# The first entry's norm moved ahead of the border between two stages of a decoder kernel

## The chip, the cores and the metric

The kernel runs on one core of one Trainium2 chip. The metric is device time in microseconds (us), from several runs; beside it stands one profiled execution, whose trace gives every instruction of every engine. The engines are TensorE (PE: matrix products and transposes; its weight loads are listed apart as PEld), VectorE (DVE), ScalarE (ACT), GpSimd (POOL) and the DMA queues, most of them fed by SyncE (SP). Each engine takes its own instructions in order and waits on semaphores for the others.

## The reference

Two decoder layers work on x of shape 8 x 256 x 256 (eight entries b of 256 tokens, width 256) with a context ctx of 8 x 256 x 512. All in float32. In short:

```python
x = x + attn0(layernorm(x))                   # 16 heads of 16, rotary
x = x + xattn0(ctx, layernorm(x))             # keys and values are halves of ctx
x = x + experts0(layernorm(x))                # 8 experts, sinkhorn gates, top 32 tokens each
x = x + attn1(layernorm(x))                   # 16 heads of 16, rotary, causal
x = x + xattn1(layernorm(x), ctx)             # 16 heads of 64, projections of ctx, a null key
x = x + ffn1(layernorm(x))                    # top 1 of 8 experts plus a shared one

def layernorm(x):
    return (x - mean(x)) / sqrt(var(x) + 1e-5)

def xattn1(xn, ctx):
    q, (k, v) = xn @ Wq, split(ctx @ Wkv)     # 256 -> 1024, 512 -> 2 x 1024
    k, v = concat(null_k, k), concat(null_v, v)
    out = softmax(q k^T / 8) v @ Wout         # per head
    return layernorm(out, 1e-6) * ln_scale + ln_bias
```

The change lies where attn1 of the last entry ends and xattn1 of the first entry begins.

## The kernel before, in words

The tokens of an entry lie as two tiles of 128 partitions; `x` holds all of them in SBUF (`x[:, 2 * b + t, :]` is tile t of entry b).

**First stage.** 24 units run one behind the other: self attention and cross attention of layer 0, entry pair by entry pair (units 0 to 15), and the causal self attention of layer 1 (units 16 to 23, one per entry). The first layer's experts run as generators between them. A unit has four steps k (two groups of heads by two tiles of keys); in step (n, k) the main loop issues the scores of the next step, then a first list of small jobs, then `values(k)` (products of exponentials and values, line 367; behind an odd k `divided_T`, lines 383 to 393, turns and divides them on DVE), then a second list. The lists are the table `order_of_jobs`, and its order is the order on all engines: the stage is traced under `manual_schedule(engines=PINNED)`, PINNED being PE, DVE, ACT, POOL and SP. The jobs kx0 to kx3 and vx0 already compute the key products of the second stage for entry 0 (`keys_x`, copied by ACT at line 888) and the first of four parts of the value products (`vals_x`, product at line 278, copied by ACT at line 902). Part 1 stands behind the loop, then the output product of the last unit (`units[-1].out`, product line 278, residual add line 502), then parts 2 and 3. After that the pinned order is closed, and the first stage's memory pools: `aw` (called `work`, with tags such as `xn` and `xnT` in two buffers), `pads`, and the PSUM pools (`amm`, called `mm`: three banks). New pools of the second stage take their room.

**Second stage.** `null_cross_attention` computes xattn1 entry by entry. Its pool `d2` is again called `work`, its PSUM pool `xmm` is again `mm`. Only PE's order is written out here; a planner orders the other engines by simulated times. It starts with `layernorm_T(0, ...)`: statistics on DVE (lines 249, 250, 252), a power -1/2 on POOL (254), two scalings on DVE (258), four transposes on PE (287), a copy by ACT (290). Then `features` (products with wq_x, PE line 272, copies by ACT at line 1404), `tables_x` (byk and its sums on DVE, lines 829 and 836; nvs zeroed by POOL at line 847 and filled by DVE at 850; nvw on PE at line 856), `null_key`, and the differences of weights on DVE (`sums_of_weights`, line 1428) that the entries from 1 on need, since their projections are made with seven products instead of eight (`seven`). Then for each entry `weighted`: scores on PE (1535), exponentials on ACT (1539, four buffers), on POOL the sum of the two key tiles (`both`, line 1541), on PE the denominators from it (`den`, line 1550) and the value products (`ox`, line 1575), whose copies alternate between ACT and DVE (1583). The order on PE is: scores of four heads pairs ahead, then the `den` products of the block before, then `ox`. The pool `kvs` on the right side of SBUF holds keys and values of one entry; it is opened at step (20, 1), together with the loads of the second stage's weights.

**Third stage.** `token_experts` runs the last feed-forward with experts loaded by DMA per slot.

Of the kernel before, what the change touches and what calls it, by code (L numbers as in the profile page):

```python
# [29 lines left out]
F32 = mybir.dt.float32  # L30
# [9 lines left out]
P = 128  # L40
B, S, D = 8, 256, 256
# [116 lines left out]
def plain(  # L158
# [7 lines left out]
    small = ctx.enter_context(tc.tile_pool(name="small", bufs=4))  # L166
# [3 lines left out]
    x = const.tile([P, NT, D], F32, name="x")  # L170
# [58 lines left out]
    def pack(e):  # L229


        full, tail = FF // P, FF % P
        to = packs[e, :, : 2 * FIRST].rearrange("p (c f) -> p c f", c=2)
        w1, w3 = (a[f"L1_ffn_{n}_eDF"][e].rearrange("(c p) f -> p c f", p=P) for n in ("w1", "w3"))
        nc.sync.dma_start(to[:, :, :FF], w1)
        nc.sync.dma_start(to[:, :, FF : FF + tail], w3[:, :, full * P :])
        nc.sync.dma_start(to[:, :, FF + tail :], w3[:, :, : full * P])
        to, w2 = packs[e, :, 2 * FIRST :].rearrange("p (c d) -> p c d", d=D), a["L1_ffn_w2_eFD"][e]
        nc.sync.dma_start(to[:, :full, :], w2[: full * P].rearrange("(c p) d -> p c d", p=P))
        nc.sync.dma_start(to[:tail, full, :], w2[full * P :])  # L240


    def norm_stats(views, eps, pool, tag):

        n = len(views)
        st = pool.tile([P, 2, 6], F32, tag=f"{tag}st", name=f"{tag}st")
        mv = pool.tile([P, 2, 2], F32, tag=f"{tag}mv", name=f"{tag}mv")
        for i, v in enumerate(views):
            nc.vector.bn_stats(st[:, i, :], v)
            nc.vector.bn_aggr(mv[:, i, :], st[:, i, :])  # L250
        ve = pool.tile([P, 2], F32, tag=f"{tag}ve", name=f"{tag}ve")
        nc.vector.tensor_scalar(ve[:, :n], mv[:, :n, 1], eps, None, ALU.add)  # L252
        rs = pool.tile([P, 2], F32, tag=f"{tag}rs", name=f"{tag}rs")
        nc.gpsimd.tensor_tensor(rs[:, :n], ve[:, :n], mhalf[:, :n], ALU.pow)  # L254
        return mv, rs

    def normed(dst, src, mv, rs, i, engine=nc.vector):
        return engine.tensor_scalar(dst, src, mv[:, i, 0:1], rs[:, i : i + 1], ALU.subtract, ALU.mult)

    def layernorm_T(b, work, mm, bufs=2):  # L260

        xn = work.tile([P, 2, D], F32, tag="xn", name="xn", bufs=bufs)
        mv, rs = norm_stats([x[:, 2 * b + t, :] for t in range(2)], 1e-5, small, "ln")
        for t in range(2):
            last = normed(xn[:, t, :], x[:, 2 * b + t, :], mv, rs, t)
        return last, transposed(xn, work, mm, "xnT", bufs=bufs)
# [9 lines left out]
    def product4(out, lhsT, rhs, start, stop):  # L276
        for h in range(0, P, HP):
            nc.tensor.matmul(  # L278
                out[h : h + HP], lhsT[:, h : h + HP], rhs, start=start, stop=stop, skip_group_check=True
            )  # L280

    def transposed(rows, work, mm, tag, dst=None, bufs=2):

        ps = mm.tile([P, 2, 2 * P], F32, tag="mm", name="tr")
        for t in range(2):
            for c in range(2):
                nc.tensor.transpose(ps[:, c, t * P : (t + 1) * P], rows[:, t, c * P : (c + 1) * P], ident)
        if dst is None:
            dst = work.tile([P, 2, 2 * P], F32, tag=tag, name=tag, bufs=bufs)
        nc.scalar.copy(dst, ps)  # L290
        return dst
# [285 lines left out]
    work = first.enter_context(tc.tile_pool(name="aw", bufs=2))  # L577
    banks = ExitStack()
    mm = banks.enter_context(tc.tile_pool(name="amm", bufs=3, space=PSUM))
# [27 lines left out]
    def expert_tables():  # L607
        nc.sync.dma_start(gate, a["L0_ffn_gate_w"].rearrange("(c p) e -> p c e", p=P))
        nc.sync.dma_start(experts, a["L0_ffn_experts"].rearrange("e (c p) f -> p e c f", p=P))

    def zeros():
        zero = one.tile([P, D], F32, name="zero")
        nc.gpsimd.memset(zero, 0.0)
        nc.sync.dma_start(xs.rearrange("(s p) d -> p s d", p=P), zero.unsqueeze(1).to_broadcast([P, TILES, D]))
        nc.sync.dma_start(
            ye[COMMON * P :].rearrange("(s p) d -> p s d", p=P), zero.unsqueeze(1).to_broadcast([P, TILES - COMMON, D])
        )
        nc.sync.dma_start(yo.rearrange("(s p) d -> p s d", p=P), zero.unsqueeze(1).to_broadcast([P, TILES - COMMON + 1, D]))
        for e in range(E):
            nc.sync.dma_start(packs[e, FF % P :, 2 * FIRST + FF // P * D :], zero[FF % P :])  # L620
# [251 lines left out]
    def context(b):  # L872
        t = ctxs.tile([P, CTX // P, S], F32, tag="ctxT", name="ctxT")
        nc.sync.dma_start(t, a["ctx_T"][b].rearrange("(c p) t -> p c t", p=P))
        return t

    def key_room():
        return kvs.tile([P, nc8, S], F32, tag="kT", name="kTx")

    def value_room():  # L880
        return kvs.tile([P, 2, XH, XD], F32, tag="vx", name="vx")
# [8 lines left out]
    def vals_x(v, ctxT, i):  # L890
        t, hh = i // 2, 8 * (i % 2)
        ps = mm.tile([P, 8, XD], F32, tag="mm", name="vps")
        lo = (XH + hh) * XD
        for cc in range(CTX // P):
            product4(
                ps.rearrange("p h d -> p (h d)"),
                ctxT[:, cc, bass.ts(t, P)],
                wkv_x[:, cc, lo : lo + 8 * XD],
                cc == 0,
                cc == CTX // P - 1,  # L900
            )
        nc.scalar.copy(v[:, t, hh : hh + 8, :], ps)
# [126 lines left out]
    def run(n, k, late):  # L1029
        for job in slots[4 * n + k][late]:  # L1030
            jobs[job]()
# [27 lines left out]
    for n, u in enumerate(units):  # L1059
        if n == 1:  # L1060
            nc.sync.dma_start(sin1, a["sin_halves"].rearrange("(t p) d -> p t d", p=P))
            expert_tables()
        if n == 3:
            zeros()
        if n == 2:
            nc.sync.dma_start(wqkv1, a["l1_wqkv"].rearrange("(c p) f -> p c f", p=P))
            nc.sync.dma_start(wo1, a["l1_wo"].rearrange("(c p) f -> p c f", p=P))
        for m in range(n + 2, min(n + 6, len(units))):
            v = units[m]
            if m == n + (5 if v.__class__ is SelfAttention else 2) or not n and m < 5:  # L1070
                v.load()
        if n >= 4 and n % 2 == 0 and n < 20:
            pack(n // 2 - 2)
        for k in range(4):
            if k < 3:
                u.core.scores(k + 1)
            elif n + 1 < len(units):
                units[n + 1].core.scores(0)
            run(n, k, 0)
            u.core.values(k)  # L1080
            run(n, k, 1)
            if (n, k) == (20, 1):
                for left in ex:
                    assert next(left, None) is None
                wd, ctxs, kvs, wproj, wkv_x, wq_x, wout_x, nkrow, nvcol, lns, lnb = weights_x()
                ctxT0, kv0 = context(0), (key_room(), value_room())
        opening.close()
    vals_x(kv0[1], ctxT0, 1)
    for t in range(2):
        units[-1].out(t)  # L1090
    for i in (2, 3):
        vals_x(kv0[1], ctxT0, i)
    order.close()
    first.close()
    banks.close()
# [1 line left out]
    mm = banks.enter_context(tc.tile_pool(name="xmm", bufs=3, space=PSUM))  # L1097
# [189 lines left out]
    def routed_norm(b, work):  # L1287

        xn = work.tile([P, 2, D], F32, tag="y", name="xne", bufs=1)
        mv, rs = norm_stats([x[:, 2 * b + t, :] for t in range(2)], 1e-5, small, "ln")  # L1290
        for kept, v in zip(norms[b], (mv, rs)):
            nc.gpsimd.tensor_copy(kept, v)
        for t in range(2):
            normed(xn[:, t, :], x[:, 2 * b + t, :], mv, rs, t)
        return xn
# [94 lines left out]
    def null_cross_attention(phase):  # L1390
        work = phase.enter_context(tc.tile_pool(name="d2", bufs=2))
# [14 lines left out]
        def query_room():  # L1406
            return work.tile([P, nc8, S], F32, tag="qT", name="qTx", bufs=1)
# [291 lines left out]

        order = ExitStack()  # L1700
        order.enter_context(tc.manual_schedule(engines={mybir.EngineType.PE}))
        _, xnT = layernorm_T(0, work, mm, 1)
        (kT, v), qT = kv0, query_room()
        features(qT, wq_x, xnT, nc.scalar.copy)
        wn, nvw, hot8 = tables_x(wd, wq_x, wout_x, nkrow, nvcol, work, mm)
# [8 lines left out]
        for b in range(B):  # L1714
# [4 lines left out]
            if more:  # L1719
                _, xnT = layernorm_T(b + 1, work, mm, 1)  # L1720
# [25 lines left out]
            rs, old = reciprocals(b, den, en), en  # L1746
# [30 lines left out]
        with tc.manual_schedule(engines={mybir.EngineType.PE, mybir.EngineType.DVE}):  # L1777
            for i, _ in enumerate(quarter(1)):
                if i == 0:
                    xn = routed_norm(B - 1, work)  # L1780
# [7 lines left out]
    with ExitStack() as phase:  # L1788
        null_cross_attention(phase)
# [1217 lines left out]
```

## Time and profile before

| what | us |
|---|---|
| median of 3 runs | 1139.07 (1138.89 to 1139.7) |
| profiled execution | 1139.85 |
| its span, first to last instruction | 1138.0 |
| PE busy | 1096.0 (96%) |
| DVE busy | 613.5 (54%) |
| ACT busy | 450.9 (40%) |
| POOL busy | 427.4 (38%) |
| granted PE clock, mean | 0.994 of full speed |
| end of the last value product of the first stage | 430.78 |
| start of the first product of the features | 432.94 |

Lines of the profile read: start, length (both us), engine, line of the kernel, operation, output<-inputs with shapes, and how many instructions are merged into the line. In brackets stands the idle time ahead of it on its engine and which instruction ended it. Summaries of a line give the least, median and largest duration in ns.

### The profile page before, as it was taken

Reading aid. Unit: us, or ns where it says so; the run is one execution under the profiler, and the core shown is the slowest. Engines: PE = TensorE matmul, PEld = TensorE weight load, DVE = VectorE, ACT = ScalarE, POOL = GpSimd, SP = SyncE. Lnnn points to the kernel's source line nnn. Section 1 sums busy time; section 2 is a strip of 40 time slices with the busy share of each in tenths; the row PEclk is TensorE's granted clock in tenths of the full one; section 3 lists DMA queues with packets and bytes.
Section 4 is the critical chain, followed back from the end, with each engine's and each line's share of the span. In section 5 each row is a group of like instructions: output and inputs, shape, how many; then the busy total and the mean of one; then the engine's idle time right before and its main releaser. Section 6 shows DMA issues by size and latency. Waiting matters only on the chain. (4 is left out here: it accounts for less than half of the span.)

```text
span 1138.0 us, 34797 instructions
## 1 busy us (share of the span) xinstructions
PE 1096.0 (96%) x15154; PEld 718.0 (63%) x15154; DVE 613.5 (54%) x1645; ACT 450.9 (40%) x727; POOL 427.4 (38%) x488
## 2 busy tenths in 40 slices
PE   6979999999999999999999999999999999999996
PEld 3434455555555445676777777777775768888874
DVE  5557889899878438344434343525257672221213
ACT  4657776656444433232323232323233320232220
POOL 3436366446677423333333424242425133000013
PEclk9989999999999999999999999999999999999998
DMA  8082333231103300102010102010122045899924
GB/s 248 2 262 101 105 107 97 75 110 55 37 12 136 118 3 20 39 20 49 20 48 20 49 20 49 20 49 20 48 104 69 1 155 206 351 412 409 375 81 130
DMA packets 54754, 120.37 MB, mean 106 GB/s; under 512 B 9008, under 2 KB 38944, under 8 KB 50240
## 3 DMA queue, kind: packets, MB, share of 16 engines
q1 hardware_dynamic: 48416, 102.32, 26.3%
q0 software_dynamic: 3456, 12.73, 3.0%
q10 hardware_dynamic: 2720, 3.02, 0.8%
q8 instruction: 121, 1.98, 0.7%
q14 instruction: 41, 0.34, 0.1%
HBM read 105.83 MB, written 29.51 MB: 119 GB/s over the span
## 5 line engine op out<-in xcount | busy, mean ns | idle before, releaser
L341 ACT ACTIVATE pT<-st 128x1024 f32<-128x1024 f32 (+1 forms) x128 | 110.4, 915 | 74.0 <-PE st L330 70.1
L367 PE MATMUL o<-pT,padv 128*32 128x256 f32 (+1 forms) x1536 | 96.4, 367 | 7.1 <-DVE by_q L383 5.6
L1541 POOL TENSOR_TENSOR both<-pTx 128x512 f32<-128x512 f32 x64 | 87.4, 1393 | 21.0 <-ACT pTx L1539 19.1
L272 PE MATMUL h<-xrT,w 128*64 128x128 f32 (+1 forms) x1936 | 86.9, 250 | 1.5 <-issue 1.5
L272 PEld LDWEIGHTS h<-xrT,w 128*64 128x64 f32 x1936 | 84.3, 137 | 4.4 <-issue 2.1
L1170 DVE TENSOR_TENSOR midr<-sl,h 128x128 f32<-128x128 f32 x102 | 29.4, 288 | 101.0 <-PE h L272 68.8
L341 ACT ACTIVATE pT<-st,kbias 128x1024 f32<-128x1024 f32 x64 | 67.8, 1111 | 36.0 <-PE st L330 36.0
L367 PEld LDWEIGHTS o<-pT,padv 128*32 128x32 f32 x1536 | 44.6, 110 | 54.7 <-issue 19.1
L1539 ACT ACTIVATE pTx<-stx 128x1024 f32<-128x1024 f32 x64 | 62.5, 1023 | 31.7 <-PE stx L1535 28.4
L1169 ACT ACTIVATE sl<-h 128x128 f32<-128x128 f32 (+1 forms) x114 | 35.2, 310 | 95.9 <-PE h L272 56.8
L254 POOL TENSOR_TENSOR lnrs<-lnve,mhalf 128x2 f32<-128x2 f32 x48 | 35.5, 743 | 94.2 <-DVE lnve L252 86.6
L330 PE MATMUL st<-qm,kT 32*128 32x512 f32 (+1 forms) x512 | 66.8, 589 | 3.9 <-DVE seq L513 2.1
L278 PE MATMUL qk<-xnT,l_wqkv 128*32 128x256 f32 x1024 | 66.9, 384 | 0.0
L1535 PE MATMUL stx<-qTx,kTx 64*128 64x256 f32 x512 | 64.4, 391 | 2.1 <-ACT pTx L1539 2.1
L1575 PE MATMUL ox<-pTx,vx 128*32 128x256 f32 x1024 | 63.3, 380 | 0.0
L1630 POOL TENSOR_TENSOR oT<-oT,rs 128x512 f32<-128x512 f32 x30 | 37.2, 1271 | 62.5 <-DMA rs<-rd 62.5
L1535 PEld LDWEIGHTS stx<-qTx,kTx 64*128 64x128 f32 x512 | 46.1, 186 | 20.4 <-issue 7.0
L346 POOL TENSOR_SCALAR_AFFINE_SELECT pT<-pT 128x512 f32<-128x512 f32 x64 | 42.1, 672 | 41.5 <-ACT pT L341 41.2
L254 POOL TENSOR_TENSOR lxrs<-lxve,mhalf 128x2 f32<-128x2 f32 x8 | 5.6, 705 | 127.3 <-DVE lxve L252 127.3
L383 DVE STREAM_TRANSPOSE by_q<-o 128x512 f32<-128x512 f32 x48 | 34.0, 708 | 33.0 <-PE o L367 32.9
L1583 DVE COPY oT<-ox 128x512 f32<-128x512 f32 x16 | 11.0, 690 | 72.3 <-PE ox L1575 72.3
L1575 PEld LDWEIGHTS ox<-pTx,vx 128*32 128x32 f32 x1024 | 35.0, 110 | 21.4 <-issue 2.7
(394 smaller groups left out, 2280.3 us busy)
## 6 DMA issues: line engine op xcount, KB each, us to landing
w<-packs SPq DMA_DIRECT2D x22, 1408.0 KB, 7.9
w<-packs SPq DMA_DIRECT2D x22, 768.0 KB, 9.3
rs<-rd SPq DMA_DIRECT2D x16, 512.0 KB, 5.9
packs<-L_ffn_w_eDF SPq DMA_DIRECT2D x8, 704.0 KB, 7.6
packs<-L_ffn_w_eDF SPq DMA_DIRECT2D x8, 640.0 KB, 7.7
packs<-L_ffn_w_eFD SPq DMA_DIRECT2D x8, 640.0 KB, 8.1
wkv_x<-L_xattn_Wkv POOLq DMA_DIRECT2D x1, 4096.0 KB
ctxT<-ctx_T SPq DMA_DIRECT2D x8, 512.0 KB, 3.9
```

The source lines that it names most:

```text
L254: nc.gpsimd.tensor_tensor(rs[:, :n], ve[:, :n], mhalf[:, :n], ALU.pow)
L272: nc.tensor.matmul(out[h], lhsT[:, h], rhs, start=start, stop=stop, skip_group_check=True)
L278: nc.tensor.matmul(out[h : h + HP], lhsT[:, h : h + HP], rhs, start=start, stop=stop, skip_group_check=True)
L330: nc.tensor.matmul(st[:, r, :, :n], self.kT[rows, c, bass.ts(kt, P)], self.qm[rows, :, c, q0:], start=True, stop=True,)
L341: nc.scalar.activation(pT[:, :, :, :n], st[:, 2 * k : 2 * k + 2, :, :n], AF.Exp, scale=self.scale, **kb)
L346: nc.gpsimd.affine_select(out=pT[:, :, :, :P], in_=pT[:, :, :, :P], compare_op=ALU.is_ge, fill=0.0, base=0, pattern=[[0, 2], [0, 2], [1, P ...
L367: nc.tensor.matmul(o[HP * j : HP * j + HP, m, q0:], self.v_pad[:, kt, 8 * c + 2 * j + m, :], pTs[j // 2][:, j % 2, m, : S - q0], start=kt ...
L1535: nc.tensor.matmul(st[:, g, kt, :], kT[rows, c, bass.ts(kt, P)], qT[rows, c, :], start=True, stop=True)
L1539: nc.scalar.activation(pT, st, AF.Exp, scale=scale)
L1541: nc.gpsimd.tensor_tensor(both, pT[:, :, 0, :], pT[:, :, 1, :], ALU.add)
L1575: nc.tensor.matmul(o[at : at + HP, i, :], v[:, kt, 2 * (c2 + i) + g, lo : lo + HP], pT[:, g, kt, :], start=kt == 0, stop=kt == 1, skip_gro ...
L1630: engines[c2 % 4 // 2].tensor_tensor(oT[:, c2 : c2 + 2, :], oT[:, c2 : c2 + 2, :], rs[:, c2 : c2 + 2, :], ALU.mult)
```

## The change

The norm of entry 0 is taken out of the second stage and written into the pinned order of the first. Its statistics are issued behind step (23, 0) of the main loop, its two scalings behind step (23, 1), into a tile `xn0` of the first stage's pool `work` (tag `xn`). Its four transposes and their copy are issued between the parts 2 and 3 of the value products, with a PSUM bank of the first stage's `mm`; the result `xnT0` lies in the pool `kvs`, which grows by one tile of 2 KB per partition. The second stage takes `xnT0` as it is. `norm_stats`, `normed` and `transposed` are the helpers that `layernorm_T` calls too; the number of instructions stays the same.

```diff
             run(n, k, 0)
             u.core.values(k)
             run(n, k, 1)
+            if (n, k) == (23, 0):
+                xn0 = work.tile([P, 2, D], F32, tag="xn", name="xn")
+                mv, rs = norm_stats([x[:, t, :] for t in range(2)], 1e-5, small, "ln")
+            if (n, k) == (23, 1):
+                for t in range(2):
+                    normed(xn0[:, t, :], x[:, t, :], mv, rs, t)
...
     for t in range(2):
         units[-1].out(t)
-    for i in (2, 3):
-        vals_x(kv0[1], ctxT0, i)
+    vals_x(kv0[1], ctxT0, 2)
+    xnT0 = transposed(xn0, kvs, mm, "xnT0", bufs=1)
+    vals_x(kv0[1], ctxT0, 3)
     order.close()
     first.close()
     banks.close()
...
-        _, xnT = layernorm_T(0, work, mm, 1)
+        xnT = xnT0
         (kT, v), qT = kv0, query_room()
         features(qT, wq_x, xnT, nc.scalar.copy)
```

## The prediction

> **What bounds the kernel now.** I read the page's first two parts, then the stretch that the change touches (420 to 465 us), engine by engine in the timeline, then TensorE's waits behind it, and the idle time of the engines that the moved work goes to.
>
> Page, busy time by engine, and two rows of the table of busy time by stage (second stage, entries 1 and 2):
> ```profile
> PE 1096.0 (96%) x15154; PEld 718.0 (63%) x15154; DVE 613.5 (54%) x1645; ACT 450.9 (40%) x727; POOL 427.4 (38%) x488
> ...
> 500.00:558.00 58.00, 57.74 (x782) 42.41 (x780) 25.99 (x69) 18.74 (x31) 19.98 (x21) 1.00 0.13 34
> 558.00:616.00 58.00, 57.74 (x780) 42.43 (x780) 24.23 (x59) 18.77 (x30) 20.20 (x21) 1.00 0.13 34
> ```
> In the rows by stage: window, its length, then busy us (and instructions) of PE, its weight loads, DVE, ACT, POOL, then granted clock and DMA. TensorE (PE) is the bound: 57.74 of 58 us in every entry of the second stage, granted clock 1.00. Whatever moves PE's work in the first entry moves the end by as much, as long as PE then waits for nothing else.
>
> Timeline of PE at the border of the stages:
> ```profile
> 422.00 1.91 PE L278 MATMUL ao<-l_wo,attT 128*32 128x256 f32 x32
> 423.73 7.05 PE L278 MATMUL vps<-wkv_x,ctxT 128*32 128x512 f32 x64
> 431.48 0.66 PE L287 MATMUL tr<-ident,xn 128*128 128x128 f32 x4 [0.71 <-ACT vx L902]
> 432.94 7.13 PE L272 MATMUL fm<-xnT,wq_x 128*64 128x256 f32 x64 [0.80 <-ACT xnT L290]
> ```
> The last two parts of the value products are the 7.05 us; they end at 430.78 and the features start at 432.94. Between lie 0.71 us of waiting, 0.66 of transposes, 0.80 of waiting.
>
> ACT beside it (copies of the value parts 2 and 3, then of the transposes):
> ```profile
> 427.41 0.59 ACT L902 COPY vx<-vps 128x512 f32<-128x512 f32 x1 [4.58 <-PE vps L278]
> 430.84 0.58 ACT L902 COPY vx<-vps 128x512 f32<-128x512 f32 x1 [2.85 <-PE vps L278]
> 432.30 0.58 ACT L290 COPY xnT<-tr 128x512 f32<-128x512 f32 x1 [0.87 <-DVE tw L1428]
> ```
> Timeline of DVE from the last residual add on, and of POOL:
> ```profile
> 423.98 0.69 DVE L502 TENSOR_TENSOR x<-x,ao 128x512 f32<-128x512 f32 x1 [3.21 <-PE ao L278]
> 424.58 1.91 DVE L258 TENSOR_SCALAR xn<-x,lnmv,lnrs 128x256 f32<-128x256 f32 x2
> 426.41 2.35 DVE L829 TENSOR_TENSOR byk<-wq_x,nkrow 128x1024 f32<-128x1024 f32 x2
> ...
> 443.98 0.41 DVE L864 COPY nvw<-nvw 128x256 f32<-128x256 f32 x1
> ...
> 448.40 0.89 DVE L1428 TENSOR_TENSOR wout_x<-wout_x 128x128 f32<-128x128 f32 x4
> 454.11 0.69 DVE L1583 COPY oT<-ox 128x512 f32<-128x512 f32 x1 [4.83 <-PE ox L1575]
> ```
> ```profile
> 425.05 0.97 POOL L847 MEMSET nvs<- 128x1024 f32 x1
> 445.16 5.26 POOL L1541 TENSOR_TENSOR both<-pTx 128x512 f32<-128x512 f32 x1 [19.14 <-ACT pTx L1539]
> ```
> DVE runs without a gap from 423.98 to 449.29: the norm, then one stream (table products, then the differences of the weights) of 449.29 - 426.41 = 22.88 us. POOL's first pair sum takes 5.26 us where the median of its 64 is 1.278 (all instances of line 1541), and it ends at 450.42, 1.13 behind the end of that stream: while DVE runs adds of two SBUF operands back to back, POOL's add stands still.
>
> Who waits for POOL: PE behind it, and the instances of line 1541.
> ```profile
> L1541 POOL TENSOR_TENSOR both<-pTx x64: 1255/1278/5256, 445.2 to 862.5; 128x512 f32<-128x512 f32 x64
> ```
> ```profile
> 450.90 0.63 PE L1550 MATMUL den<-both,hot 128*32 128x256 f32 x4
> 451.70 0.41 PE L1550 MATMUL den<-both,hot 128*32 128x256 f32 x2 [0.17 <-POOL both L1541]
> ```
> This is the line that decides. The second pair sum ends at 450.42 + 1.25 = 451.67, and PE takes up the matmul that needs it at 451.70, after a wait of 0.17. So at 451.7 the first entry already hangs on the end of DVE's stream: PE has 0.17 us of nothing to spare there. A gain ahead of it is lost at this place unless DVE's stream ends sooner too, and a later stream costs its whole delay.
>
> **The change, part by part.**
>
> *Statistics and norm, 20 us sooner.* Statistics: DVE 2 x 0.40 (bn_stats) + 2 x 0.17 + 0.15, some 1.3 us, behind the add-up of step (23,0), where DVE has nothing between 403.47 and 411.56; POOL's power 0.7 us (684 ns median) behind the mask of 406.18, which ends at 407.41, with POOL's next work at 412.13; the two scalings 2 x 0.40 behind the residual add that ends at 414.1, with DVE's next work at 418.82. Nothing queued behind them is due. POOL's masks of 414.65 to 415.88 may hold up the scalings or be held: the value products that need the masks start at 417.27, so up to 1.4 us is covered. Cost on the path: 0. No DMA is moved; in the unpinned order of before the statistics already ran ahead of 366 us, so they take nothing off the border.
>
> *Transposes between parts 2 and 3.* Four at a total of 0.66, same as now; PE reaches them at about 427.3 and the third part ends at 430.78 + 0.66 = 431.44 (0.5 if they overlap the products better). Their copy (0.58 on ACT) lies under the third part. The context load on SP waits for the third part's end: 0.66 later, landing some 6 us behind, needed at 444.6: covered.
>
> *Features.* They no longer wait for a norm's transposes. What is late next is the copy of the third part: 431.44 + 0.06 + 0.58 = 432.08, so the features start at about 432.14 instead of 432.94: PE gains 0.80. That the first product of the second stage waits for this copy I take from the transposes of before, which stood until 431.48 for the copy that ended at 431.42, though by the tiles of the program another bank than the one copied there was theirs: the new banks wait for all of the old ones. If only one bank counted, the features would follow at 431.44 and the gain be 1.5.
>
> *DVE's stream.* The two scalings leave 424.58, so the stream could start there, 1.83 sooner. But its first writes go into rooms of the second stage, which are opened over the closed rooms of the first, and the moved rows now lie in a room of the first (tag xn), read by the moved transposes. In before the last reader of those rooms was the output product that ends at 423.91, which DVE had waited for anyway. If the new rooms wait for every reader of the old ones, DVE now stands from 424.67 until the transposes end, 427.3 + 0.66 + 0.07 = about 428.0. Queued behind: the whole stream, then POOL's pair sums, then PE. The trace of before does not show this wait, so both ends: no wait, stream at 424.67 (-1.74); full wait, stream at 428.0 (+1.6). I take the full wait: the compiled program of before lists, for the first writes into the new room, waits for the last mask on POOL and the last transposition of the heads on DVE, whose tiles lie at other addresses than those written. [...]
>
> *The sum.* DVE's stream ends at 428.0 + 22.88 = 450.9 instead of 449.29, the second pair sum at 453.3 instead of 451.67: PE's 0.80 are gone and it goes on 1.6 later than before. One relief: PE's lead brings POOL's first pair sum to 444.3, ahead of the copy of nvw (before at 443.98, then at 445.6), which reads PSUM; if POOL slips in there, it runs 1.26 us, holds DVE for 0.93, and of the two sums one is left to do behind the stream: 450.9 + 0.93 + 1.13 = 452.95, 1.3 later. I take +1.5. All behind it is PE-dense and shifts as one. Profiled execution: 1139.85 (span 1138.0 and 1.85 around it) becomes 1141.3; it lies 0.8 above the median of the runs, 1139.07, which becomes **1140.6**, +0.13%. A measurement of this kernel tells some 0.2% from no change, so this is "same".
>
> [...]
>
> **The rivals.**
>
> *A. DVE doesn't wait* (the rooms go by address, or DVE finds other work first). Stream at 424.67 to 426.4: the second sum ends at or before 451.67, PE keeps 0.2 to 0.8, up to 1.5 if the features don't wait either: 1137.6 to 1138.9, worked as 1138.3. For it: DVE is in time everywhere else; against: the wait lists above.
>
> [...]
>
> [...]
>
> *C. Another plan.* In the second stage only PE's order is written out; the planner orders the others anew. PE has at most 0.26 us of waiting per entry to give back, so a new order can gain under 2 us and lose more, for example an oT copy queued behind a product that comes late: 0.3 us an entry, eight entries, 1143.
>
> **How the numbers follow.** Forecast (+0.9 to +2.0) 0.52; A 0.20; a part of the wait, 0 to +0.9, 0.11; B 0.08; C 0.09 (0.06 of it slower). Under 1136.8 (faster by 0.2%) 0.03; over 1141.35 (slower by 0.2%): B, most of C and the upper edge of the forecast, 0.17; within 0.80. Range: from A's gain of 1.4, 1137.7, to C's 1143.0. The likeliest one's own range is 1140.0 to 1141.1.
>
> **What would show it.** Right: features start near 432.1; byk starts near 428.0, with DVE idle ahead of it and the transposes named; the first pair sums end behind the end of DVE's stream near 451; PE waits over 1 us for POOL at line 1550. Wrong: byk at 424.7 (A), byk's first product over 2 us (B), or entries of the second stage whose length is no longer 57.7 us (C).

## The result, and the profile after

| | before, us | after, us |
|---|---|---|
| median, 6 runs each | 1139.25 (1138.89 to 1140.3) | 1135.45 (1132.62 to 1136.18) |
| profiled execution | 1139.85 | 1136.18 |
| its span | 1138.0 | 1134.6 |

The ratio is 0.996, with a 95% interval of 0.9946 to 0.9973. Two repeats later, each with its own runs of the kernel before, gave 0.995 (0.9935 to 0.9965) and 0.9961 (0.9949 to 0.9973). The change made the kernel faster by 0.4 to 0.5%, 4 to 6 us; the forecast was 1140.6, slower by 1.5.

The gain lies in three stretches, and only one of them is the border. Busy time by stretch, kernel before and then changed kernel (window, its length, then busy us and instructions of PE, its weight loads, DVE, ACT, POOL, then granted clock, DMA share, GB/s):
```profile
357.00:380.00 23.00, 21.01 (x341) 10.79 (x336) 14.44 (x43) 9.64 (x17) 15.36 (x22) 1.00 0.83 311
425.00:465.00 40.00, 38.07 (x454) 22.34 (x447) 28.62 (x69) 14.74 (x20) 14.95 (x10) 1.00 0.05 15
845.00:880.00 35.00, 34.02 (x296) 18.44 (x292) 25.60 (x37) 13.58 (x17) 22.52 (x33) 1.00 0.45 139
```
```profile
357.00:380.00 23.00, 22.64 (x371) 12.12 (x364) 14.66 (x38) 11.37 (x18) 16.01 (x24) 1.00 0.72 278
425.00:465.00 40.00, 39.04 (x470) 22.61 (x462) 34.05 (x68) 14.61 (x20) 15.36 (x10) 1.00 0.05 15
845.00:880.00 35.00, 34.74 (x320) 19.82 (x318) 19.21 (x38) 14.44 (x19) 21.06 (x33) 1.00 0.46 139
```
PE is fuller in all three after the change: 22.64 of 23 us instead of 21.01, 39.04 of 40 instead of 38.07, 34.74 of 35 instead of 34.02. Between the second and the third it is as full as before.

To size them, the rest of the document uses lengths between fixed PE instructions of one profile, so that nothing depends on how late a profile is at the first of them:

- I, first stage: from the `v` product that waits for the residual add of line 779 (361.79 in before) to the output product `ao` of the last unit (422.00).
- II, border: from there to the first key product of entry 1 (460.95).
- III, the rest of the second stage: from there to the transposes of `xne` in the last entry (864.89).

| profile | I | II | III |
|---|---|---|---|
| before, first and second profile | 60.21, 60.19 | 38.95, 38.95 | 403.94, 403.95 |
| changed, three profiles | 57.87, 57.87, 57.88 | 37.43, 37.45, 37.43 | 402.49, 402.51, 402.56 |
| difference | -2.33 | -1.51 | -1.4 |

About 0.2 of the last is given back by 890 us, so the three make 2.33 + 1.51 + 1.4 - 0.2 = 5.0 us.

**Border (II).** The changed kernel, PE:
```profile
428.80 0.66 PE L287 MATMUL tr<-ident,xn 128*128 128x128 f32 x4
429.39 3.64 PE L278 MATMUL vps<-wkv_x,ctxT 128*32 128x512 f32 x32
433.73 7.13 PE L272 MATMUL fm<-xnT,wq_x 128*64 128x256 f32 x64 [0.70 <-ACT vx L902]
...
451.70 0.64 PE L1557 MATMUL den<-both,hot 128*32 128x256 f32 x8
```
DVE, and POOL:
```profile
429.55 2.36 DVE L829 TENSOR_TENSOR byk<-wq_x,nkrow 128x1024 f32<-128x1024 f32 x2 [3.36 <-PE tr L287]
...
446.53 0.68 DVE L1435 TENSOR_TENSOR wq_x<-wq_x 128x512 f32<-128x512 f32 x1
447.13 2.65 DVE L258 TENSOR_SCALAR xn<-x,lnmv,lnrs 128x256 f32<-128x256 f32 x2
449.70 1.49 DVE L1451 TENSOR_TENSOR sw<-ctxT 128x256 f32<-128x256 f32 x1
...
458.60 0.68 DVE L1590 COPY oT<-ox 128x512 f32<-128x512 f32 x1
```
```profile
445.96 6.37 POOL L1548 TENSOR_TENSOR both<-pTx 128x512 f32<-128x512 f32 x4 [15.43 <-ACT pTx L1546]
```
From `ao` (423.53 here) the features start after 10.20 us, in before after 432.94 - 422.00 = 10.94: 0.74 sooner. DVE waits 3.36 us for the moved transposes. But the `den` product at 451.70 waits for nothing: POOL's four pair sums run from 445.96 to 452.33, not behind DVE's stream, which lasts until 458.68. From the first of these `den` products to the next scores PE takes 2.29 us (451.70 to 453.99), in before 3.08 (450.90 to 453.98): that is the rest of the border's gain.

**First stage (I).** Before, POOL and PE:
```profile
364.33 2.69 POOL L254 TENSOR_TENSOR lnrs<-lnve,mhalf 128x2 f32<-128x2 f32 x4 [1.95 <-DVE lnmv L250]
367.02 2.57 POOL L258 TENSOR_SCALAR xn<-x,lnmv,lnrs 128x256 f32<-128x256 f32 x2
369.56 2.46 POOL L346 TENSOR_SCALAR_AFFINE_SELECT pT<-pT 128x512 f32<-128x512 f32 x4
```
```profile
370.29 1.44 PE L367 MATMUL o<-pT,padv 128*32 128x256 f32 x14 [1.54 <-POOL pT L346]
```
Changed kernel, the same two:
```profile
367.57 0.72 POOL L254 TENSOR_TENSOR lnrs<-lnve,mhalf 128x2 f32<-128x2 f32 x1 [1.22 <-DVE lnve L252]
368.40 2.44 POOL L258 TENSOR_SCALAR xn<-x,lnmv,lnrs 128x256 f32<-128x256 f32 x2
370.80 1.23 POOL L346 TENSOR_SCALAR_AFFINE_SELECT pT<-pT 128x512 f32<-128x512 f32 x2
```
```profile
372.42 1.05 PE L367 MATMUL o<-pT,padv 128*32 128x256 f32 x16
```
In before four powers stood on POOL ahead of the scalings of unit 23's norm and of the masks; three belong to the norms of entries 0, 1 and 2 of the second stage, whose statistics the planner had put at 362 to 366 us. With entry 0's written behind step (23, 0), all three sets run there (404.92 to 407.75 on DVE, 408.92 to 410.94 on POOL), and PE's wait is gone.

**Last entry (III).** Before, DVE, POOL and PE:
```profile
852.20 2.72 DVE L1189 TENSOR_TENSOR tws<-ws 128x640 f32<-128x640 f32 x2
854.84 3.71 DVE L1189 TENSOR_TENSOR tws<-ws,tws 128x640 f32<-128x640 f32 x2
...
864.16 1.27 DVE L1583 COPY oT<-ox 128x512 f32<-128x512 f32 x2
```
```profile
852.39 11.56 POOL L1541 TENSOR_TENSOR both<-pTx 128x512 f32<-128x512 f32 x7
```
```profile
864.01 0.63 PE L1550 MATMUL den<-both,hot 128*32 128x256 f32 x4 [0.46 <-POOL both L1541]
864.89 0.66 PE L287 MATMUL tr<-ident,xne 128*128 128x128 f32 x4 [0.26 <-DVE oT L1583]
```
Changed kernel, DVE and POOL:
```profile
856.77 0.69 DVE L1590 COPY oT<-ox 128x512 f32<-128x512 f32 x1 [4.52 <-PE ox L1582]
863.15 0.69 DVE L1590 COPY oT<-ox 128x512 f32<-128x512 f32 x1 [5.69 <-PE ox L1582]
...
864.09 0.82 DVE L1196 TENSOR_TENSOR tws<-ws 128x640 f32<-128x640 f32 x1
```
```profile
852.37 6.19 POOL L1548 TENSOR_TENSOR both<-pTx 128x512 f32<-128x512 f32 x5
859.35 2.52 POOL L1548 TENSOR_TENSOR both<-pTx 128x512 f32<-128x512 f32 x2 [0.79 <-PE den L1557]
```
The planner now puts the differences of the third stage's shared weights (`tws`, and those of `xne` behind it) after the copies of the head outputs. POOL's sums are no longer stretched by them (11.56 / 7 = 1.65 us each before, 1.24 and 1.26 after), and PE waits for neither. That its simulated times were shifted is the likely reason for the new order, but no run tests it.

**What is left of the profiles.** By these lengths the profiled executions should differ by 5.0 us and differ by 3.7. Two things that come and go between executions of the same kernel make up the rest. The changed kernel's profile has two stretches of 5 us with a mean granted clock of 0.66, at 20 and 290 us, and before's first profile has none there. By 27 us PE is 2.3 behind that profile (0.9 of it already ahead of the stretch at 20 us), and the second stretch costs 1.6 more: 3.9. At the end, the first add of `out` to x comes 1125.09 - 1118.47 = 6.6 us behind the start of the last products in before and 1120.22 - 1117.33 = 2.9 in the changed kernel, which with the adds and stores behind it shortens that profile by 2.3 more. -5.0 + 3.9 - 2.3 = -3.4, which is the difference of the spans, 1134.6 - 1138.0. The repeats show both things in both kernels (below).

### The profile page after: what moved, and what is told of

Same layout as the page of the kernel before. It is cut to its first block, busy times and chain, and to the rows that moved or that the text cites. A ratio compares the mean times of both kernels' runs of the same rounds, so it can differ in the third digit from the quotient of the medians.

```text
span 1134.6 us, 34799 instructions
## 1 busy us (share of the span) xinstructions
PE 1098.1 (97%) x15154; PEld 718.4 (63%) x15154; DVE 613.2 (54%) x1645; ACT 450.7 (40%) x727; POOL 426.6 (38%) x488
## 4 chain that ended last, share of the span: by engine, by line
PE 87%; DVE 6%; ACT 3%; issue 1%; SPq 1%; DMA 1%; POOL 0%; ACTq 0%; DVEq 0%; POOLq 0%
PE h L272 7%; PE st L330 7%; PE k L272 7%; PE v L272 6%; PE o L367 5%; PE ox L1582 5%; PE stx L1542 5%; PE wo L272 4%; PE out L2002 4%; PE out L1819 4%; PE qk L278 4%; PE h L1184 3%; PE q L272 3%; PE ao L278 2%; ACT pT L341 2%; PE v L278 2%
## 5 line engine op out<-in xcount | busy, mean ns | idle before, releaser
L1548 POOL TENSOR_TENSOR both<-pTx 128x512 f32<-128x512 f32 x64 | 84.1, 1341 | 19.5 <-ACT pTx L1546 15.4
L278 PEld LDWEIGHTS qk<-xnT,l_wqkv 128*32 128x32 f32 x1024 | 32.9, 113 | 27.0 <-issue 9.2
```

The costliest lines, as they stand in the source:

```text
L278: nc.tensor.matmul(out[h : h + HP], lhsT[:, h : h + HP], rhs, start=start, stop=stop, skip_group_check=True)
L1548: nc.gpsimd.tensor_tensor(both, pT[:, :, 0, :], pT[:, :, 1, :], ALU.add)
```

## The experiments

The theory after the comparison: three gains that are independent of each other, of which the border's is the smaller part. Rivals: all of it is made at the border; the first and third stretch are chance; and, for the border itself, the wait of DVE that the prediction saw is harmless in general, or only just missed.

### The changed kernel and the kernel before once more

No edit.

> The changed kernel once more, with a second profile. Theory 1 (three gains that belong to the program): 2.45 us of PE between 360 and 380 us, 1.5 between 427 and 455, 1.46 in the last entry of the second stage of which 0.3 are given back, all there again in the second profile; about 4.6 us off the kernel before in a profile without the two stretches of granted clock 0.66 (20 to 25 and 290 to 295 us), about 3 to 4 in the median. Theory 2 (what the first two profiles differ in is mostly chance from run to run): the gain between 360 and 380 us or that in the last entry isn't there again, and the ratio is above 0.998. The end of the third stage, where the first profile was 2.2 us shorter, I expect to differ between two profiles of this same kernel by as much.

> The changed kernel once more, on the same chip and beside the two kernels below. With the gains found so far (2.3 in the first stage, 1.5 at the border, 1.2 in the last entry) 5.0 us of PE less than before, a ratio of 0.9955 to 0.9965 or a little lower. If the ratio is above 0.998, the gains don't reach the whole time.

> The kernel before, one more profile. PE's wait of 1.5 us near 370, that of 0.46 at the last entry's denominators, the stretched first pair sum of 5.3 us, and nothing of PE's own times moved by over 0.1 us between the stretches of lower granted clock. Whether it has the stretch at 20 us, I take as chance: if so, 2.3 us more than its first profile.

Measured: 1136.37 against 1142.24 for the kernel before (0.995), 1135.13 against 1139.02 (0.9961); the kernel before took 1138.70 in one further profiled execution, span 1136.8. That is 5.9 and 3.9 us less for the changed kernel, the first of them more than the 3 to 4 expected. The lengths I to III agree to 0.07 us between profiles of the same kernel (table above), so the three gains are the program's. The stretch of 0.66 at 20 us is in all three profiles of the changed kernel and in the second of before, where PE is 2.1 late by 27 us (expected 2.3). That at 290 us is in two of three of the changed kernel and in neither of before. The delay of the first add at the end: 6.6 and 2.9 us in the two profiles of before, 2.9, 6.9 and 2.9 in those of the changed kernel.

### The statistics alone, the last entry's order alone, and both

Statistics alone:
```diff
             u.core.values(k)
             run(n, k, 1)
+            if (n, k) == (23, 0):
+                first_norm = norm_stats([x[:, t, :] for t in range(2)], 1e-5, small, "ln")
...
-        _, xnT = layernorm_T(0, work, mm, 1)
+        xn0 = work.tile([P, 2, D], F32, tag="xn", name="xn", bufs=1)
+        for t in range(2):
+            normed(xn0[:, t, :], x[:, t, :], *first_norm, t)
+        xnT = transposed(xn0, work, mm, "xnT", bufs=1)
```


> The kernel before, with only the statistics of the first entry's norm put behind step (23, 0); scalings and transposes stay in the second stage. Theory 1: the statistics (and with them those of the next two entries) no longer run ahead of 366 us, POOL has one power there in place of three, and PE's wait for POOL near 370 us goes: 2.45 us less, 1136.8 where the kernel before has 1139.25. The border and the last entry stay as in before. Rival (my prediction: the early statistics cost nothing, the gain is made at the border): 0, 1139.25.

The last entry's order alone (`sx` differences likewise):
```diff
-            nc.vector.tensor_tensor(r, den, en, ALU.add)
+            shared["den"] = nc.vector.tensor_tensor(r, den, en, ALU.add)
...
-                shared["of_w"] = sums_of_shared(...)
+                with tc.issue_after(shared["den"].ins):
+                    shared["of_w"] = sums_of_shared(...)
```


> The kernel before, with only the differences of the shared weights and of x, for the next stage, made to wait for the last sum of the denominators, so that DVE's order in the last entry of the second stage is that of the changed kernel. Theory 1: the copies of the head outputs come sooner, POOL's pair sums are not stretched, and PE gains 1.1 to 1.5 us between 848 and 885: 1137.8 to 1138.2 where the kernel before has 1139.25. Rival (the differences are only moved, and the next stage waits for them): 0, or up to 1 us slower.

Both of these edits:

> The kernel before with both of these edits; every engine's order is then that of the changed kernel, but for the scalings, transposes and copy at the border. Theory 1 (the gains add up): 2.45 + 1.1 to 1.5 less than before, 1135.3 to 1135.7, and the changed kernel lies 1.5 below that. Rival (the border gives nothing that lasts, as my prediction had it): the changed kernel lies at this kernel's time or 1.5 above it.

| kernel | time, us | ratio to 1142.24 | I | II | III |
|---|---|---|---|---|---|
| statistics alone | 1139.99 | 0.9981 (0.9968 to 0.9993) | 57.87 | 38.96 | 403.92 |
| last entry alone | 1140.74 | 0.9989 (0.9979 to 0.9999) | 60.19 | 38.95 | 402.58 |
| both | 1139.01 | 0.9972 (0.9960 to 0.9984) | 57.87 | 38.95 | 402.58 |
| changed kernel | 1136.37 | 0.9950 (0.9935 to 0.9965) | 57.87 | 37.45 | 402.51 |

Each edit moves its own stretch, by the whole of what the change moves it, and no other. In time the first is worth 2.3 us (expected 2.45), the second 1.5 (expected 1.1 to 1.5), both 3.2 (expected 3.6 to 3.9, within the interval). What the changed kernel has beyond both is the border: 2.6 us in time, 1.5 in the profile. So by the lengths 3.5 of the 5.0 us have nothing to do with transposes or features, in time 3.2 of 5.9. What in the rest of the change makes the planner reorder the last entry was not tested; the statistics alone do not (III 403.92).

### What in the first stage costs: the statistics or the powers

The changed kernel with its statistics where before had them:
```diff
+            if (n, k) == (20, 2):
+                mv, rs = norm_stats([x[:, t, :] for t in range(2)], 1e-5, small, "ln")
             if (n, k) == (23, 0):
                 xn0 = work.tile([P, 2, D], F32, tag="xn", name="xn")
-                mv, rs = norm_stats([x[:, t, :] for t in range(2)], 1e-5, small, "ln")
```


> The changed kernel, with the statistics of the first norm put back to where they ran before, behind step (20, 2); the two other entries' statistics follow them there. Border and last entry as in the changed kernel. Theory 1 (the first stage's gain comes from the statistics and powers leaving that place): TensorE's wait for POOL near 370 us is back, 2.3 us of PE are lost between 360 and 380, and the kernel lies 2.3 above the changed one, at a ratio of about 0.997 to the kernel before. Rival (the gain in that stretch has another source, chance in the release of masks for one): the same time as the changed kernel, 0.995.

The changed kernel with three more powers between the one of unit 23 and its scalings:
```diff
+    def powers():
+        spent = small.tile([P, 2], F32, tag="dp", name="dp", bufs=1)
+        for _ in range(3):
+            nc.gpsimd.tensor_tensor(spent, units[23].rs, mhalf[:, :2], ALU.pow)
+    jobs["dp0"] = powers
...
-        | st23 va22 no23 vb21
+        | st23 dp0 va22 no23 vb21
```


> The changed kernel, with three more powers of the same shape on POOL behind the one of the last unit; their results aren't used, DVE's order is untouched, and no statistics are moved. Theory 1a (POOL's powers ahead of the masks are the cost; 0.7 us each): masks 2.1 later, PE waits about 1.4 for the transposed exponentials, 1.5 to 2.4 us above the changed kernel. Theory 1b (DVE's ten instructions of statistics are the cost): no loss, within 0.2 us of the changed kernel.

The first missed: I is 58.26, so 0.39 of the 2.33 comes back (time 1137.57, ratio 0.9966, 0.9953 to 0.9978, measured without the changed kernel beside it). Its POOL:
```profile
365.28 0.73 POOL L254 TENSOR_TENSOR lnrs<-lnve,mhalf 128x2 f32<-128x2 f32 x1 [1.22 <-DVE lnve L252]
366.12 2.44 POOL L258 TENSOR_SCALAR xn<-x,lnmv,lnrs 128x256 f32<-128x256 f32 x2
368.53 0.71 POOL L254 TENSOR_TENSOR lnrs<-lnve,mhalf 128x2 f32<-128x2 f32 x1
369.21 1.24 POOL L346 TENSOR_SCALAR_AFFINE_SELECT pT<-pT 128x512 f32<-128x512 f32 x2
```
Here the statistics and powers run as early as in before, but the unit's own power and scalings come first on POOL, and the others between and behind the masks. The second kernel puts them ahead again: I is 59.83, 1.96 of the 2.33, PE waits 1.18 us at 371.65 for the masks (time 1138.97, 0.9974, 0.9961 to 0.9988). So what cost 2.33 us was not that the powers ran there: it was that three of them, 0.7 us each, stood on POOL ahead of the scalings and of all four masks. The 0.4 that remain were not taken apart.

The second kernel also missed by 1.1 us at the border (II 38.58): DVE's stream there ended 2.0 us later than in the changed kernel (460.70 against 458.68), and PE waited for the copy behind it:
```profile
456.02 3.87 DVE L1441 TENSOR_TENSOR two<-wout_x,two 128x128 f32<-128x128 f32 x8
```
```profile
461.35 0.66 PE L287 MATMUL tr<-ident,xn 128*128 128x128 f32 x4 [1.07 <-DVE oT L1596]
```
Those eight took 1.69 in the changed kernel. POOL's last two sums, in the changed kernel and then in this one:
```profile
456.70 4.34 POOL L1548 TENSOR_TENSOR both<-pTx 128x512 f32<-128x512 f32 x2 [1.34 <-PE den L1557]
```
```profile
456.54 2.59 POOL L1554 TENSOR_TENSOR both<-pTx 128x512 f32<-128x512 f32 x2 [1.34 <-PE den L1563]
```
In both kernels they start 0.52 behind the eight (456.70 and 456.18, here 456.54 and 456.02); there POOL was held up, here DVE. In all three profiles of the changed kernel, and in that with the early statistics, the first of these sums took 3.11 to 3.12 us; here it took 1.30, and the add of DVE that started 0.08 behind it took 1.37 in place of 0.28. Whether the three powers or chance decided it, one profile cannot tell. The changed kernel's border stands that near to a wait.

### The border, taken apart

Rows in the pool of the keys (DVE need not wait for the transposes), transposes behind the fourth value part, and both:
```diff
-                xn0 = work.tile([P, 2, D], F32, tag="xn", name="xn")
+                xn0 = kvs.tile([P, 2, D], F32, tag="xnT0", name="xn0", bufs=1)
...
-    xnT0 = transposed(xn0, kvs, mm, "xnT0", bufs=1)
+    xnT0 = transposed(xn0, kvs, mm, "", xn0)
```


> The changed kernel, with the scaled rows of the first norm in the pool of the keys in place of the first stage's pool, so that no room that the second stage's tables take is still read by the transposes. DVE's first table product then starts near 426.4 in the time of the changed kernel's profile instead of 429.55, and its stream ends some 3 us sooner. Theory 1 (the wait of DVE that my prediction saw is real and harmless, since POOL gets in between): PE's times as in the changed kernel, within 0.1 us. Rival (the pair sums hang on the stream's end, as my prediction had it, or POOL gets in only because the stream is late): PE's wait for POOL at the denominators changes, by -0.3 to +0.8 us.

> The changed kernel with the scaled rows in the pool of the keys, once more, beside the changed kernel itself. PE's times were the same at the border, so the same time, within 0.1%. Rival: DVE's stream, 14 us shorter in time there, gives something behind the border that one profile didn't show: 1 us or more less than the changed kernel; or the ratio of 0.9966 in the earlier call, 1.8 us above that of the changed kernel in its own, is real.

```diff
-    vals_x(kv0[1], ctxT0, 2)
-    xnT0 = transposed(xn0, kvs, mm, "xnT0", bufs=1)
-    vals_x(kv0[1], ctxT0, 3)
+    for i in (2, 3):
+        vals_x(kv0[1], ctxT0, i)
+    xnT0 = transposed(xn0, kvs, mm, "xnT0", bufs=1)
```


> The changed kernel, with the four transposes behind the fourth value part in place of ahead of it; their bank is still the first stage's. PE then transposes without a wait, but the copy of the transposes comes behind that of the fourth part on ScalarE, so the features start as early as in the changed kernel (0.0 to 0.1 later): the gain of 0.7 before the features comes from the bank, not from the place between the parts. DVE's stream starts later by the fourth part and the copy, 2.1 us. Theory 1 (POOL and VectorE alternate once POOL is in): PE's times within 0.2 us of the changed kernel. Rival (my prediction: each us that the stream is later is paid by PE at the denominators): up to 2 us slower than the changed kernel.

> Both edits at once: the transposes behind the fourth value part, and the scaled rows in the pool of the keys. With the transposes last alone, the kernel lost 5 to 7 us against the changed one. Theory (that loss comes from DVE's tables waiting for the transposes of rows that lie in a first-stage room, and then the copy of the head outputs behind DVE's stream): DVE's stream now starts near 423 in the time of that profile and all of the loss goes; the features start as early as in the changed kernel or 0.1 sooner, so 0 to 0.2 us from the changed kernel. Rival (the place of the transposes itself costs, through ScalarE's copies or the banks): 2 us or more above the changed kernel.

Two sets of measurements stand in this table. Compare times only within a set: 1143.53 and 1137.22 belong to one in which the kernel before took 1141.86, the others to one in which it took 1139.02. The ratios can be compared across both.

| transposes | rows | time, us | ratio to before | II |
|---|---|---|---|---|
| between the parts | first stage's pool (changed) | 1135.13 | 0.9961 | 37.43 |
| between the parts | pool of the keys | 1134.94; 1137.22 | 0.9962; 0.9966 | 37.44; 37.43 |
| behind part 4 | first stage's pool | 1143.53 | 1.0005 (0.9993 to 1.0018) | 41.99 |
| behind part 4 | pool of the keys | 1135.19 | 0.9962 (0.9949 to 0.9974) | 37.27 |

Transposes last, rows in the first stage's pool: DVE, POOL (one line of a narrow window) and PE:
```profile
446.55 2.64 DVE L258 TENSOR_SCALAR xn<-x,lnmv,lnrs 128x256 f32<-128x256 f32 x2
...
460.18 1.28 DVE L1590 COPY oT<-ox 128x512 f32<-128x512 f32 x2
```
```profile
441.78 5.98 POOL L1548 TENSOR_TENSOR both<-pTx 128x512 f32<-128x512 f32 x1 [11.84 <-ACT pTx L1546]
```
```profile
449.09 0.41 PE L1557 MATMUL den<-both,hot 128*32 128x256 f32 x2 [0.65 <-POOL both L1548]
...
460.91 0.66 PE L287 MATMUL tr<-ident,xn 128*128 128x128 f32 x4 [3.09 <-DVE oT L1590]
```
Transposes last, rows in the pool of the keys: DVE, POOL and PE:
```profile
424.27 2.35 DVE L829 TENSOR_TENSOR byk<-wq_x,nkrow 128x1024 f32<-128x1024 f32 x2
```
```profile
443.95 4.33 POOL L1548 TENSOR_TENSOR both<-pTx 128x512 f32<-128x512 f32 x1 [18.23 <-ACT pTx L1546]
```
```profile
449.69 0.64 PE L1557 MATMUL den<-both,hot 128*32 128x256 f32 x8
```
The place between the parts brings nothing by itself: with the rows out of the first stage's room, the transposes may come last and II is even 0.16 shorter. What brings the first 0.74 is that the transposes no longer wait in PE's queue for the copy of the fourth part: with both edits they stand behind that part and start without a wait, and the features come 10.04 us behind `ao` (10.94 in before). The wait of DVE is real and can cost much: where its stream starts 3.4 us later, counted from `ao` (transposes last, rows in the first stage's room; I had expected 2.1), PE waits 0.22 and 0.65 at the denominators and 3.09 for a copy of the head outputs behind the stream, and the gain of the change is lost in the median (the runs lie between 1138.89 and 1145.11). At the border it is 4.6 us more than in the changed kernel, which missed both sides of the expectation, 0.2 and 2. In the changed kernel the wait costs nothing: without it II is the same. There, with the rows in the pool of the keys, DVE's stream ends 9.7 us sooner, counted from `ao`, and is 6.3 us shorter (not 14, as an expectation above has it), and POOL again stands until its end: its first sum takes 4.16. None of the three variants is faster than the changed kernel beyond the intervals. The later start and the wait in the changed kernel are thus free only because the transposes stand ahead of the fourth part.

## Why the prediction was wrong

*Features 0.80 sooner, held by the copy of the last value part (part 3, the fourth):* right, 0.74, and PE names that copy (0.70 at 433.73).

*DVE's stream waits for the moved transposes, to about 428.0:* right. `byk` starts at 429.55, and the profile was 1.53 late at `ao`: 428.02 in the time of before. The two edits of the room confirm the cause. Rival A, no wait, is out for the changed kernel, and rival B, the zeroing of nvs holding up `byk`, too (B had it from a scaling of 1.59 us beside the zeroing in before, where others took 0.40): the first two products of `byk` take 2.36 us beside the zeroing of nvs at 429.58, as in before (2.35).

*"A later stream costs its whole delay", second pair sum at 452.95 to 453.3:* this step failed. I took the first pair sum's 5.26 us in before as a law, POOL stands still until the stream's end, with the copy of nvw as the only way in. In the changed kernel the second sum ends at 449.64, or 448.1 in the time of before: over 4.8 us ahead of the forecast. POOL gets in where DVE changes from its adds to the two scalings of entry 1's norm (line 258). In before these ran ahead of POOL's first sum at 445.16:
```profile
443.66 0.40 DVE L258 TENSOR_SCALAR xn<-x,lnmv,lnrs 128x256 f32<-128x256 f32 x1
443.98 0.41 DVE L864 COPY nvw<-nvw 128x256 f32<-128x256 f32 x1
444.31 0.40 DVE L258 TENSOR_SCALAR xn<-x,lnmv,lnrs 128x256 f32<-128x256 f32 x1
```
In the changed kernel they are 1.9 later (1.6 from the wait, the rest from the copy of nvw, now ahead of them) and PE 0.7 earlier, so the sum was there first, at 445.96 against 447.13. As long as its sums follow each other, POOL is not pushed out again: until 455.4 each takes 1.3 to 1.5, and all but one of DVE's operations 1.36 to 1.50 instead of 0.28 to 0.41. After a pause it is held once more, until the stream's end (the sum at 456.70). No row shows POOL getting in at the copy of nvw, nor the 0.93 us that it was to hold DVE for there in the forecast's sum: that copy ended at 444.20, ahead of POOL's first sum, and the rows show 0.96 to 1.09 more for each of DVE's operations that was held. DVE pays for the sums, but what stands behind its stream, the copy of head outputs that ends at 459.28, is needed only by the transposes at 460.38. So the late stream did no harm, where I had it cost PE 0.80 and 1.3 to 1.6 more. Nor is it needed for the second gain of 0.77: with the rows in the pool of the keys POOL's sums do hang on the stream's end, as I had it, but that end comes 1.83 us sooner behind `ao` than in before, and II is the same 37.43. I had also read the wait of 0.17 at 451.70 as all that PE loses to POOL there. It loses 0.79, 3.08 against 2.29 us from the first `den` product to the next scores.

*"In the unpinned order of before the statistics already ran ahead of 366 us, so they take nothing off the border" and cost 0:* right for the border, and the largest miss all the same, 2.33 us. I costed their new place and not what they had held up in the old one. The line of POOL with four powers at 364.33 and PE's wait of 1.54 at 370.29 were in the profile of before.

*Rival C, another plan by the planner, "can gain under 2 us":* it did, 1.4 in the last entry, of which 0.2 were given back. I named it, but with 0.09, and mostly as a loss, and did not look for a place where the order could improve. The 0.26 us of waiting per entry that I worked with hold for the entries 1 to 6; the last entry had 0.98 (35.02 of 36 us busy from 848 to 884). The pair of DVE's `tws` at 852 ahead of a copy that PE waits for at 864.89 was there to be found.

With the border alone the time would have been 1.5 lower by the lengths. That is the figure of rival A's best case, but by luck: A had it from features that do not wait, and they wait. The other 3.5 us came from engines' orders far from the border.

## What to carry to other kernels

Work that is moved leaves a place as well as taking one: price what stood behind it in its old place, on each engine's queue, and look there for a wait of the bounding engine. Where only part of the order is written out, a change in one place reorders another, so compare the whole order of each engine, and look ahead of time for waits elsewhere that a new order could end. A wait that costs nothing in one arrangement can cost over 4 us in the next (II of 37.43 and 41.99): the pool that a tile lies in decided here whether the place of the instruction mattered.

## What the runs showed of the hardware

*When POOL gets in beside DVE.* In the first profile of before, POOL's first sum ends 1.13 us behind the end of DVE's stream (450.42 and 449.29). Where the stream still has scalings to come, the sum ends the same time behind the start of the first scaling: 448.34 - 447.13 = 1.21 in the changed kernel, 447.76 - 446.55 = 1.21 with the transposes last (1.14 behind the stream's end where both edits leave it no scaling to come), although it had been waiting 1.2 and 4.8 us, past adds that started after it. So in these rows the earlier start did not help POOL among adds that follow each other without a gap, and what ended the wait was the first scaling or the stream's end. That is not a law either. With the three added powers, the sum at 456.54 got in among adds, with no other operation of DVE near, and took 1.30 us, where the sum at the same place was held in four other profiles (3.11 to 3.12).

*The clock.* Beside the stretch from 75 to 85 us, where its mean is 0.66 in the first profile of before and 0.68 in that of the changed kernel, the granted clock falls in some executions and not in others, behind a wait of PE. Over a window of 5 us that holds the whole stretch its mean is 0.66; from 290.3 to 293.7 us of the changed kernel's first profile it is 0.50. Rows of one stretch, first profile of before and then of the changed kernel:
```profile
290.00:295.00 5.00, 5.00 (x112) 2.93 (x112) 4.19 (x13) 4.13 (x7) 4.04 (x5) 1.00 0.02 5
```
```profile
290.00:295.00 5.00, 5.00 (x65) 2.11 (x64) 3.59 (x13) 1.46 (x3) 3.87 (x4) 0.66 0.03 8
```
65 products instead of 112. These are not the same products, since the changed kernel is 2.3 us later there; its second profile, which reaches the place at the same time, has 116 at a clock of 1.00. Over all 14 profiles, it is there at 285 to 295 in 6, where the mean from 285 to 297 us is 0.86 and 1.00 in the others (the wait ahead of it was 1.48 to 1.76 us in the 6, 0.55 to 1.49 in the others). It is there at 20 to 25 in 8: behind a wait of 1.88 to 2.16 us, 32 products of line 278 take 2.53 to 3.60 us in these, and 1.93 in the other 6, behind one of 2.15. It costs 1.6 and 1.4 us where two profiles of one kernel differ in it. With the transposes last, the wait of 3.09 at the border was followed by a mean of 0.83 at 460 to 470 that cost 1.6 more (III of 404.12 there instead of 402.5). What sets it off was not shown: at 290 us it follows waits of 1.48 and 1.49 in two profiles (early statistics; rows in the pool of the keys, the second) and does not follow one of 1.49 in two others (last entry alone; both). Whether the change itself makes the stretch at 290 us more frequent (2 of 3 profiles against 0 of 2) stays open; it would have cost, not gained.

*The end of the kernel.* The first add of `out` comes 2.9 us behind the start of the last products in 5 of the 14 profiles and 6.5 to 6.9 in 9, in both kernels; the last add then ends 11.0 or 12.0 to 12.3 us behind that start. What delays it was not tested.
